# A graph layer on one core: groups of six edges, one-hots of 128 columns, and fields turned a row later

## The chip, the cores and the metric

The kernel runs on one core of a Trainium2 chip. The metric is the device time of one execution in microseconds (us). The core has a matrix engine (TensorE, PE in the profile, with its weight loads listed apart as PEld), a vector engine (VectorE, DVE), a scalar engine (ScalarE, ACT), GpSimd (POOL) and a queue engine (SyncE, SP). Each engine runs its own instructions in order and waits on semaphores for the others.

## The reference

There are 625 nodes with 512 numbers each, and 20,625 edges, sorted by the node they end at (`dst`), each with a source node, one of four types and a weight.

```python
h = relu(layernorm(x))
xs = h[src]
for r in range(4):
    w_r = where(edge_type == r, edge_weight, 0.0)
    total_msg += (xs @ W_rel[r] + b_rel[r]) * w_r[:, None]
agg = segment_sum(total_msg, dst) / maximum(segment_sum(edge_weight, dst), 1.0)
x1 = layer_norm(h + h @ W_self + b_self + agg, ln1_g, ln1_b)
ffn = gelu(x1 @ W_ffn1 + b_ffn1) @ W_ffn2 + b_ffn2
out = x + layer_norm(x1 + ffn, ln2_g, ln2_b)
```

The feed-forward layer is 512 to 1024 to 512.

## The kernel before

**Table.** The 625 nodes are five blocks of 125. For each type `r` and block `i`, `table_rows(r, i)` (L366) multiplies the block's 125 rows of `h` by `W_rel[r]`: four f32 matmuls of 128x128 by 128x512, each done as two passes and so shown as two records. ScalarE scales the result (L374) and a DMA on SP's queue writes it to a table in DRAM (L376). There are 4 x 5 = 20 such rows of the table; the loop over `(r, i)` runs through them in order. What is to be summed for a node is then a weighted sum of rows of this table.

**Two ways to sum.** For blocks 0, 1 and 2 (called outer or dense) the weights are made into a dense matrix: `turn_fields(d)` (L597) turns the edges' fields of outer block `d` with five bf16 matmuls against an identity; `slot_hots(d, u)` makes, on VectorE, the one-hot matrices of a unit of 16 slots: `low` (L614; which of 125 rows, with one more column of ones, so 126 columns), `eq` (L617) and `high` (L620, three of them). `slot_sums` (L631) multiplies `low` by `high`: a bank is four matmuls, each with a weight load of its own (126 columns that stand 8 elements of bf16 apart, so 16 bytes) and 120 moving columns. `empty_sums` (L637) adds a bank up into `sums_w` on VectorE. An outer block has 4 units of 4 banks: 12 units, 48 banks and 192 matmuls in all. `chunk_sum` (L1043) then multiplies `sums_w` by table rows, 20 for each outer block; nine of them are kept in SBUF and eleven are read back from DRAM (`tr`, two to a load).

For blocks 3 and 4 (called inner) the table's rows are gathered edge by edge. `gather` (L919) is an indirect DMA on GpSimd's queue that brings 128 table rows of 2 KB to 128 partitions. Edges of the inner part are put into groups of 128 x EG, where each partition holds EG edges that follow one another, so nearly always edges of one node. The first of the EG gathered rows is scaled by ScalarE into PSUM (`first_row`, L925), the others are added by VectorE (`row_added`, L943), and the sum goes through one matmul with a one-hot of the destination node (`edge_sum`). This matmul is in plain f32 (two passes, L966), or, for a parted sum, two faster matmuls of a high and a low half (L963, L964) after one more operation on ScalarE (`high`, L929) and one on VectorE (`low`, L933). Where a partition holds edges of two nodes, the later ones are left out and added from a second gather for the inner block's nodes: EG - 1 gathers for a block (`gather_first`, L973; `add_first`, L969).

**Order.** In the first part (the loop over `(r, i)`) the order is written out by hand: units of `slot_hots` are interleaved with rows of the table, up to `PER_ROW` = 3 banks behind a row; `EARLY` units are done there, the rest later. In the second part `Plan` orders the work: a list scheduler that runs at build time on costs in the code (a gather is 1.3, a bank 0.33, a pause of GpSimd after every `RUN` = 4 gathers 0.5) and emits a fixed order for each engine. It places the products with `W_self` (`pz`, L386), the chunk sums, the edge sums, the layer norms, the transposes (L319) and the feed-forward matmuls (`pu` L714, `po` L732). The feed-forward layers run in the order of blocks 0, 1, 3, 2, 4. At most `MS` = 8 gathered tiles, two PSUM tiles for edge groups (`add`) and six `es` tiles are there at a time.

The diff touches these places: the constant `EG`; the tiles `lows` and their constant fill (L292); the matmul of `slot_sums`; the constants `PARTED`, `FIRST_AT` and `EARLY`; and the conditions in the loop over `(r, i)` that say behind which row the fields are turned and the weights of the slots and the degrees are made.

Of the kernel before, what the change touches and what calls it, by code (L numbers as in the profile page):

```python
# [12 lines left out]
BF16 = mybir.dt.bfloat16  # L13
# [1 line left out]
ALU = mybir.AluOpType  # L15

P = 128
EG = 3
SLOTS = 64


class EdgePlan:
# [3 lines left out]
    def __init__(self, n_nodes, n_tiles, n_free, nb):  # L26
# [21 lines left out]
        tiles = [j for j in range(n_tiles) if window[j][1] > n0 and window[j][0] < n1]  # L48
        self.groups = -(-len(tiles) // EG)
        self.group0 = min(tiles[0], n_tiles - EG * self.groups)  # L50
        self.limits = [(0, b0 * P) if j < self.group0 else ((b1 + 1) * P, nb * P) for j in range(n_tiles)]
        self.of_sum = {}
        for k in range(self.groups):
            unit = list(range(self.group0 + EG * k, self.group0 + EG * (k + 1)))
            lo, hi = self.row(window[unit[0]][0]), self.row(window[unit[-1]][1] - 1)
# [3 lines left out]
            else:  # L59
                limits = (bs[0] * P + P // 2, bs[1] * P + P // 2)  # L60
                assert len(bs) == 2 and limits[0] <= lo and hi < limits[1]
            self.limits[unit[0]:unit[-1] + 1] = [limits] * EG
            self.of_sum.setdefault(bs, []).append(unit)
# [73 lines left out]
def gnn_layer(ctx, tc, x, edges, edge_groups, firsts, fourths, windows, w_self, w_rel, w_ffn1, w_ffn2, brel_in, rows_in, bf1_in, out, n_edges):  # L137
# [12 lines left out]
    nc = tc.nc  # L150
# [10 lines left out]
    NG = ep.each  # L161
# [7 lines left out]
    SL = windows.shape[1] // 4  # L169
# [11 lines left out]
    mid = ctx.enter_context(tc.tile_pool(name="mid", bufs=1))  # L181
# [71 lines left out]
    xw = const.tile([P, 4, INNER], F32, name="xw")  # L253
    x_cols = const.tile([P, INNER, EG, 3], F32, name="x_cols")
    x_on = const.tile([P, INNER, EG - 1], F32, name="x_on")
    x_step = const.tile([P, INNER, EG, 2], F32, name="x_step")
# [14 lines left out]
    TB = 8  # L271
    TP = 2
# [1 line left out]
    grid = mid.tile([P, NG, TB], BF16, name="grid")  # L274
    keys = mid.tile([P, 2 * NC, TP], BF16, name="keys")
    ident_b = early.tile([P, P], BF16, name="ident_b")
    lows = [mid.tile([P, SL // 4 // TB, NG + 1, TB], BF16, name=f"low_{n}") for n in range(2)]

    def node_constants():
        place = early.tile([P, 1], F32, name="place")  # L280
        nc.gpsimd.iota(place, pattern=[[0, 1]], base=0, channel_multiplier=1, allow_small_or_imprecise_dtypes=True)
        nc.gpsimd.memset(node_f, 2.0 * N)
        nc.gpsimd.memset(xw, -1.0)
        for b in range(NB):
            n = ep.size[b]
            nc.vector.tensor_scalar(node_f[:n, at_of[b]:at_of[b] + 1], place[:n], float(ep.first[b]), None, op0=ALU.add)
            if b in inner:
                nc.vector.tensor_scalar(xw[:n, 0, b - B0:b - B0 + 1], place[:n], float(b * P), None, op0=ALU.add)
        nc.gpsimd.iota(keys, pattern=[[1, 2 * NC], [0, TP]], base=0, channel_multiplier=0,
                       allow_small_or_imprecise_dtypes=True)  # L290
        for t in lows:
            nc.gpsimd.memset(t[:, :, NG:, :], 1.0)  # L292
        nc.gpsimd.iota(grid, pattern=[[1, NG], [0, TB]], base=0, channel_multiplier=0,
                       allow_small_or_imprecise_dtypes=True)

# [294 lines left out]
    QT = 4  # L590
    UNIT = SL // 4
# [31 lines left out]
    def slot_sums(d, u, q, low, high, place):  # L623
        if (d, u, q) == (d, 0, 0):
            sums_w[OUTER[d]] = const.tile([P, NC, P], F32, tag="sums_w", name=f"sums_w{d}", bufs=2)
        pool, tag = place
        p = pool.tile([P, D], F32, tag=tag, name=f"bank_{d}_{u}_{q}")
        W = 3 * 2 * NC
        for i in range(QT):
            t = q * QT + i  # L630
            nc.tensor.matmul(p[:NG + 1, i * W:(i + 1) * W], low[:, t // TB, :, t % TB], high[:, t // TP, :, t % TP],  # L631
                             start=True, stop=True)
        return p

# [160 lines left out]
    PAUSE = 200  # L795
    RUN = 4
    LATER = 0.3
    PARTED = 1, 2
    LA = 3
    CH = 2  # L800
    FIRST_AT = (2, 3)
    units = [(d, u) for d in range(ND) for u in range(SL // UNIT)]
    EARLY = 7
    PER_ROW = 3
    with tc.manual_schedule(engines={PE, DVE, ACT, mybir.EngineType.Pool}):
        nc.scalar.activation(gelu_of, ones, AF.Gelu)
        node_constants()
        stats = x_stats(0)

        def next_norm(i):  # L810
            nonlocal stats
            if i < NB:
                pre_norm(i, stats)
            if i + 1 < NB:
                stats = x_stats(i + 1)

        warm = ps_one.tile([P, D], F32, tag="one", name="warm")
        for _ in range(WARM):
            nc.tensor.matmul(warm, zeros[:, :P], zeros, start=True, stop=True)
        next_norm(0)  # L820
        for k, n in ((0, 1), (1, 1), (2, 2)):
            transposed(hT[0][:, k:k + n, :], z[:, 0, k * P:(k + n) * P], f"h0_{k}")
        next_norm(1)
        hots, waiting, later, sums_now = {}, units[:EARLY], [], []
        for r in range(R):
            for i in range(NB):
                def next_transposed():
                    transposed(hT[i + 1], z[:, i + 1, :], f"h{i + 1}")
                    next_norm(i + 2 if i == 0 else i + 3)

                table_rows(r, i, next_transposed if r == 0 and i + 1 < NB else None)
                for d, u, q in sums_now:
                    p = slot_sums(d, u, q, *hots[d, u], ((ps_one, "one"), (ps_acc, "acc"), (ps_add, "add"), (ps_add, "add"))[q % 4])
                    empty_sums(d, u, q, p)
                sums_now = [later.pop(0) for _ in range(min(PER_ROW, len(later)))]
                if r == 0 and i < 3:
                    if i == 0:
                        next_norm(3)
                        find_tiles()
                    rows_of_tiles(2 * i, min(2 * i + 2, NB))  # L840
                if (r, i) == (0, 3):
                    find_windows()
                if (r, i) == (1, 0):
                    edge_columns()
                if (r, i) == (1, 1):
                    slot_weights(0, ND)
                    slot_fields()
                if (r, i) == (1, 4):
                    slot_weights(ND, NB)
                    slot_degrees()  # L850
                    degrees_turned = relation_degrees()
                if (r, i) == (2, 2):
                    degrees_turned()
                if (r, i) >= (1, 3) and waiting and len(later) + len(sums_now) <= UNIT // QT:
                    d, u = waiting.pop(0)
                    if d not in turned_fields:
                        turn_fields(d)
                    hots[d, u] = slot_hots(d, u)
                    later += [(d, u, q) for q in range(UNIT // QT)]
                if (r, i) == (1, NB - 1):  # L860
                    group_columns()
                if r == 3 and i < KD:
                    nc.vector.tensor_add(ws_sb[:, i, i * P:(i + 1) * P], ws_sb[:, i, i * P:(i + 1) * P], ident)
                if (r, i) == (3, 0):
                    for g_bc in (g1_bc, g2_bc):
                        nc.vector.tensor_scalar(g_bc, g_bc, 1.0 / RS, None, op0=ALU.mult)
                if (r, i) == FIRST_AT:
                    first_edges()
                    load_first_edges()
                if (r, i) == (2, NB - 1):  # L870
                    set_limits(0)
                    set_limits(1)
                    total_outside = count_outside()
            later_loads(r)
        assert not waiting
        for d, u, q in sums_now + later:
            p = slot_sums(d, u, q, *hots[d, u], ((ps_one, "one"), (ps_acc, "acc"), (ps_add, "add"), (ps_add, "add"))[q % 4])
            empty_sums(d, u, q, p)
        for d in range(ND):
            if d not in turned_fields:  # L880
                turn_fields(d)
# [101 lines left out]
    g_last, g_before, n = None, None, 0  # L983
# [62 lines left out]
    m, ld, t, here = {b: None for b in OUTER}, None, None, {}  # L1046
# [19 lines left out]
    stay, i = list(range(NC - KEPT, NC)), 0  # L1066
    for d, b in enumerate(OUTER):
        weights_of(d)
        order = (*stay, *range(NC - KEPT)) if d != 1 else (*range(NC - KEPT), *stay)
        for c in order:  # L1070
            if c not in stay and (b, c) not in here:
                n = min(CH, NC - KEPT - c)
# [8 lines left out]
            if i == 8:  # L1081
                t = op("PE", 0.1, lambda: total_outside(), after=[m[b], first_ready], take=["ps"], give=["ps"], lag=2.0, rank=(2, 2.085))
# [15 lines left out]
    for b in range(NB):  # L1098
# [3 lines left out]
        for name, eng, us, fn, needs in steps:  # L1102
# [4 lines left out]
        p = [None]  # L1107
        t = op("PE", 0.46, lambda got=got, p=p, b=b: p.__setitem__(0, turn(got["x1"], f"x1_{b}")),
               after=[made["x1"]], take=["ps"], give=["ow"], rank=(1,))
# [5 lines left out]
    for blocks in together:  # L1115
        members, n = [], 0
# [177 lines left out]
```

## Time and profile before

| | |
|---|---|
| median of 3 runs | 303.15 us (300.43 to 304.28) |
| profiled execution | 304.07 us, of which the profile's span is 302.2 us |
| PE busy | 283.5 us (94% of the span) |
| DVE busy | 188.5 us (62%) |
| POOL busy | 102.3 us (34%) |
| ACT busy | 60.1 us (20%) |
| DMA | 47.94 MB, 159 GB/s over the span |
| mean granted TensorE clock | 0.977 |

The profile is of one execution. Its groups of instructions give for a line the count, the busy time and the mean duration; matmuls overlap, so the mean of one is longer than the distance between two. The chain of waits follows the work that ended last back through what released it; there, pieces of work stand end to end.

### The profile page before, as it was taken

Reading aid. Unit: us, or ns where it says so; the run is one execution under the profiler, and the core shown is the slowest. Engines: PE = TensorE matmul, PEld = TensorE weight load, DVE = VectorE, ACT = ScalarE, POOL = GpSimd, SP = SyncE. Lnnn points to the kernel's source line nnn. Section 1 sums busy time; section 2 is a strip of 40 time slices with the busy share of each in tenths; the row PEclk is TensorE's granted clock in tenths of the full one; section 3 lists DMA queues with packets and bytes.
Section 4 is the critical chain, followed back from the end, with each engine's and each line's share of the span. In section 5 each row is a group of like instructions: output and inputs, shape, how many; then the busy total and the mean of one; then the engine's idle time right before and its main releaser. Section 6 shows DMA issues by size and latency. Waiting matters only on the chain.

```text
span 302.2 us, 3190 instructions
## 1 busy us (share of the span) xinstructions
PE 283.5 (94%) x1047; PEld 174.3 (58%) x1047; DVE 188.5 (62%) x440; ACT 60.1 (20%) x115; POOL 102.3 (34%) x146
## 2 busy tenths in 40 slices
PE   7999949999999999999697979999999999999991
PEld 3444414776677575644263745685954456686870
DVE  5613179677594678974686739697979650650614
ACT  2331120111210020212021202032532001121230
POOL 6161500000300008777777474742777110000000
PEclk9999987999999999999999979999999999999997
DMA  7759765852111139668999998551567332001011
GB/s 236 293 150 342 252 210 216 313 206 63 39 36 50 49 110 282 176 170 221 297 258 291 286 257 242 150 170 35 152 193 196 120 100 72 2 0 34 2 36 37
DMA packets 19972, 47.94 MB, mean 159 GB/s; under 512 B 2351, under 2 KB 3065, under 8 KB 19824
## 3 DMA queue, kind: packets, MB, share of 16 engines
q1 hardware_dynamic: 13348, 27.54, 28.1%
q0 software_dynamic: 6304, 19.89, 23.2%
q10 hardware_dynamic: 300, 0.26, 0.4%
q8 instruction: 9, 0.15, 0.2%
q14 instruction: 11, 0.09, 0.1%
HBM read 41.29 MB, written 6.52 MB: 158 GB/s over the span
## 4 chain that ended last, share of the span: by engine, by line
PE 73%; DMA 12%; DVE 6%; issue 4%; POOL 3%; SPq 1%; DVEq 0%; POOLq 0%
PE acc L1043 14%; PE pt L366 14%; PE bank L631 12%; PE pu L714 12%; PE po L732 11%; PE pz L386 5%; DMA tr<-table 4%; DMA ms<-table,row_i 4%; PE acc L966 3%; DMA xs<-in_x_dram 2%; DMA win<-in_windows_dram,at_i 2%; POOL dst L462 2%; PE acc L960 1%; POOL win L462 1%; PE acc L964 1%
## 5 line engine op out<-in xcount | busy, mean ns | idle before, releaser
L919 POOL DMA_INDIRECT ms<-table,row_i x69 | 69.0, 1000 | 70.6 <-DVE eq L617 33.7
L366 PE MATMUL pt<-wr,hT 128*128 128x512 f32 x160 | 74.4, 614 | 0.2
L631 PEld LDWEIGHTS <-low 128*126 128x126 bf16 x192 | 48.5, 321 | 9.9 <-issue 6.4
L637 DVE TENSOR_REDUCE sums_w<-bank 126x160 f32<-126x480 f32 x48 | 31.2, 656 | 30.7 <-PE bank L631 30.7
L366 PEld LDWEIGHTS pt<-wr,hT 128*128 128x128 f32 x160 | 30.3, 197 | 33.3 <-issue 32.8
L631 PE MATMUL bank<-high,low 128*126 128x120 bf16 x192 | 44.3, 367 | 0.0
L714 PE MATMUL pu<-x1T,w_sb 128*128 128x125 f32 x320 | 37.8, 276 | 0.0
L714 PEld LDWEIGHTS pu<-x1T,w_sb 128*128 128x128 f32 x320 | 36.9, 192 | 1.4 <-issue 1.4
L1043 PE MATMUL acc<-tr,sums_w 126*128 126x512 f32 x66 | 32.7, 626 | 3.7 <-DMA tr<-table 3.7
L732 PE MATMUL po<-w_sb,gT 128*125 128x512 f32 (+2 forms) x96 | 35.7, 521 | 0.0
L925 ACT ACTIVATE ea<-ms,ed 128x512 f32<-128x512 f32 x23 | 15.9, 691 | 60.6 <-DMA ms<-table,row_i 33.4
L943 DVE SCALAR_TENSOR_TENSOR ea<-ms,wgt_g,ea 128x512 f32<-128x512 f32 x31 | 22.9, 747 | 8.0 <-DMA ms<-table,row_i 6.6
L374 ACT ACTIVATE m<-pt,rx 125x512 f32<-125x512 f32 x20 | 13.7, 687 | 70.5 <-PE pt L366 60.4
L732 PEld LDWEIGHTS po<-w_sb,gT 128*125 128x125 f32 x96 | 16.5, 188 | 15.2 <-issue 13.0
L1043 PE MATMUL acc<-m,sums_w 126*128 126x512 f32 x54 | 25.2, 596 | 0.0
L718 ACT ACTIVATE gT<-pu,bf 128x125 f32<-128x125 f32 x40 | 14.7, 366 | 46.2 <-PE pu L714 46.2
L1043 PEld LDWEIGHTS acc<-tr,sums_w 126*128 126x128 f32 x66 | 12.4, 199 | 16.3 <-issue 11.6
L740 DVE TENSOR_TENSOR y<-po,z 125x512 f32<-125x512 f32 (+2 forms) x6 | 3.6, 603 | 24.2 <-PE po L732 24.2
L386 PE MATMUL pz<-ws_sb,hT 128*128 128x512 f32 x40 | 18.1, 596 | 0.0
L1043 PEld LDWEIGHTS acc<-m,sums_w 126*128 126x128 f32 x54 | 10.0, 191 | 10.2 <-issue 10.1
L555 POOL DMA_INDIRECT x_edges<-in_edge_groups_dram,x_group x2 | 1.9, 944 | 41.2 <-DVE x_group L551 40.9
L620 DVE TENSOR_TENSOR high<-eq,turned 128x640 bf16<-128x640 bf16 x36 | 15.5, 487 | 0.4
(168 smaller groups left out, 243.2 us busy)
## 6 DMA issues: line engine op xcount, KB each, us to landing
tr<-table SPq DMA_DIRECT2D x15, 504.0 KB
table<-m SPq DMA_DIRECT2D x20, 250.0 KB
w_sb<-in_L_gnn_W_ffn_dram SPq DMA_DIRECT2D x2, 2048.0 KB
wr<-in_L_gnn_W_rel_dram SPq DMA_DIRECT2D x3, 1024.0 KB
rows<-in_rows_dram SPq DMA_DIRECT2D x1, 1536.0 KB
ms<-table,row_i POOLq DMA_INDIRECT x69, 4.1
ws_sb<-in_L_gnn_W_self_dram SPq DMA_DIRECT2D x1, 1024.0 KB
out_dram<-y SPq DMA_DIRECT2D x4, 224.0 KB
```

Of the source, the lines that this page charges most:

```text
L366: nc.tensor.matmul(p, hT[i][:, k, :], wr_sb[r][:, k, :], start=(k == 0), stop=(k == KD - 1))
L386: nc.tensor.matmul(p[0], hT[i][:, k, :], ws_sb[:, k, :], start=(k == 0), stop=(k == KD - 1))
L620: nc.vector.tensor_mul(high[:, :, a * 2 * NC:(a + 1) * 2 * NC, :], eq, pairs(2 + a))
L631: nc.tensor.matmul(p[:NG + 1, i * W:(i + 1) * W], low[:, t // TB, :, t % TB], high[:, t // TP, :, t % TP], start=True, stop=True)
L637: nc.vector.tensor_reduce(sums_w[OUTER[d]][:NG + 1, :, n0:n0 + 2 * QT].rearrange("p c (t h) -> p t h c", h=2), p[:NG + 1, :QT * 3 * 2 * NC ...
L714: nc.tensor.matmul(pu[:, :nn], w1_sb[:, k, f * P:(f + 1) * P], x1T_b()[:, k, :nn], start=(k == 0), stop=(k == KD - 1))
L718: nc.scalar.activation(box["gT"][:, f, :nn], pus[f][:, :nn], AF.Gelu, bias=bf1[:, f:f + 1])
L732: nc.tensor.matmul(po[h][:n, :w], box["gT"][:, f, at], w2_sb[:, f, c], start=(f == 0), stop=(f == KF - 1))
L919: nc.gpsimd.indirect_dma_start(out=ms[j], out_offset=None, in_=table[:, :], in_offset=bass.IndirectOffsetOnAxis(ap=row_i[:, j:j + 1], axis=0))
L925: nc.scalar.activation(box["sum"], ms[j], AF.Copy, scale=wgt[:, j:j + 1])
L943: nc.vector.scalar_tensor_tensor(to, ms[j], wgt_g[:, k, q - 1:q], box["sum"], op0=ALU.mult, op1=ALU.add)
L1043: nc.tensor.matmul(acc[b,], sums_w[b][:NG + 1, c, :], kept[(b, c) if (b, c) in kept else c][:NG + 1], start=first, stop=last)
```

## The change

Groups have six edges to a partition instead of three. `low` has 128 columns: 125 one-hot columns, one of ones, and two of zeros that are written once; the matmul takes all 128. The first fields are turned behind row (1, 4) of the table instead of (1, 3), the slot weights of the inner blocks and the degrees move from behind (1, 4) to behind (2, 0), their turned degrees from (2, 2) to (2, 3), and the first edges from (2, 3) to (2, 2). Six units instead of seven are done in the first part. The rule for parted sums changes from every second one with at least three behind it to every one with at least three behind it.

```diff
-EG = 3
+EG = 6
...
-    lows = [mid.tile([P, SL // 4 // TB, NG + 1, TB], BF16, name=f"low_{n}") for n in range(2)]
+    lows = [mid.tile([P, SL // 4 // TB, P, TB], BF16, name=f"low_{n}") for n in range(2)]
...
         for t in lows:
-            nc.gpsimd.memset(t[:, :, NG:, :], 1.0)
+            nc.gpsimd.memset(t[:, :, NG:NG + 1, :], 1.0)
+            nc.gpsimd.memset(t[:, :, NG + 1:, :], 0.0)
...
-            nc.tensor.matmul(p[:NG + 1, i * W:(i + 1) * W], low[:, t // TB, :, t % TB], high[:, t // TP, :, t % TP],
+            nc.tensor.matmul(p[:, i * W:(i + 1) * W], low[:, t // TB, :, t % TB], high[:, t // TP, :, t % TP],
                              start=True, stop=True)
...
-    PARTED = 1, 2
+    PARTED = 1, 1
     LA = 3
     CH = 2
-    FIRST_AT = (2, 3)
+    FIRST_AT = (2, 2)
     units = [(d, u) for d in range(ND) for u in range(SL // UNIT)]
-    EARLY = 7
+    EARLY = 6
...
                 if (r, i) == (1, 1):
                     slot_weights(0, ND)
                     slot_fields()
-                if (r, i) == (1, 4):
+                if (r, i) == (2, 0):
                     slot_weights(ND, NB)
                     slot_degrees()
                     degrees_turned = relation_degrees()
-                if (r, i) == (2, 2):
+                if (r, i) == (2, 3):
                     degrees_turned()
-                if (r, i) >= (1, 3) and waiting and len(later) + len(sums_now) <= UNIT // QT:
+                if (r, i) >= (1, 4) and waiting and len(later) + len(sums_now) <= UNIT // QT:
```

`PARTED` is read by `parted(k, units)`: `k % PARTED[1] < PARTED[0] and k + 3 < len(units)`, where `units` are the groups that go to one accumulator. The groups of the inner part are 23 before (11, 2 and 10 in the three accumulators) and 12 after (6, 1 and 5).

## Prediction

> **What bounds the kernel now.** I read the engines' shares first, then the chain of waits, then its pieces in order of time.
>
> ```profile
> PE 283.5 (94%) x1047; PEld 174.3 (58%) x1047; DVE 188.5 (62%) x440; ACT 60.1 (20%) x115; POOL 102.3 (34%) x146
> PE 73%; DMA 12%; DVE 6%; issue 4%; POOL 3%; SPq 1%; DVEq 0%; POOLq 0%
> ```
>
> TensorE carries the end. A busy TensorE is not one at its peak, so the pieces of the chain, which stand end to end, give the real cost of each step (start, length, what):
>
> ```profile
> 44.16 0.29 PE tf L597
> 44.44 9.47 PE pt L366 x16
> 53.91 2.59 PE bank L631 x12
> 56.50 3.49 PE pt L366 x8
> ...
> 102.83 3.49 PE pt L366 x8
> 106.32 3.52 PE bank L631 x16
> 109.83 0.28 PE tf L597 x5
> ...
> 195.56 0.74 PE bank L631 x4
> ...
> 227.57 0.23 PE acc L963
> 227.80 0.23 PE acc L964
> ...
> 242.24 0.86 PE acc L966 x2
> ```
>
> A table row is 3.49 us. A bank of four matmuls is 0.86 (2.59 / 3) in a run of three and 0.74 alone: 0.19 to 0.22 us for a weight load and a matmul with 120 columns. The five turns of the fields, which also load 128 columns of bf16 each and stream 128, take 0.28, so 0.056 apiece. The cost of a bank is thus its weight load, not its stream. Between 44.4 and 109.8 the chain is table rows and banks alone: 28 banks, 24.1 us.
>
> The rows of the windows show the parts (length from A to B, then busy time of PE, PEld, DVE, ACT and POOL):
>
> ```profile
> 44.16:110.11 65.95, 65.95 (x214) 44.39 (x215) 45.35 (x100) 9.60 (x16) 2.48 (x9) 0.96 0.35 122
> 110.11:242.30 132.19, 125.98 (x444) 75.51 (x443) 100.88 (x210) 28.08 (x52) 82.22 (x107) 0.99 0.72 205
> 242.30:295.53 53.23, 53.20 (x288) 37.31 (x286) 19.47 (x53) 11.45 (x28) 1.01 (x1) 1.00 0.12 35
> 295.53:302.20 6.67, 0.00 (x0) 0.00 (x0) 2.94 (x10) 0.20 (x1) 0.00 (x0) 0.73 0.15 42
> ```
>
> In the second, the gathers run beside TensorE. Their issues in the timeline of GpSimd:
>
> ```profile
> 112.74 1.25 POOL L919 DMA_INDIRECT ms<-table,row_i  x1 [33.70 <-DVE eq L617]
> ...
> 160.29 0.95 POOL L919 DMA_INDIRECT ms<-table,row_i  x1 [0.16 <-issue]
> ...
> 211.17 0.95 POOL L919 DMA_INDIRECT ms<-table,row_i  x1 [2.37 <-DVE ea L943]
> ...
> 234.05 0.95 POOL L919 DMA_INDIRECT ms<-table,row_i  x1 [0.16 <-issue]
> ```
>
> Numbered from 1 these are the 33rd at 160.29, the 57th at 211.17 and the 73rd, the last. The pace is 1.49 us (47.55 / 32) where nothing holds them, 2.12 (50.88 / 24) in the middle, where they wait for gathered tiles to come free, and 1.68 (121.3 / 72) over all.
>
> **The change part by part.**
>
> *One-hots of 128 columns.* The weight load is what a bank costs, and it changes from 126 columns to 128, 16 bytes apart as before. No row has a load of 128 columns at that distance. The bounds: 0.225 us for a bank, as for the turned fields, whose columns stand close together, and 0.86, no change. Below 0.225 the stream of 120 columns leaves no room, since the turns' 0.056 is for 128. I take 0.225: the same type, the same count of columns, and f32 loads of 128 columns are hidden under the matmuls in the table rows, so no load of full width shows a cost here, and only that of 126 does. The two more zero fills on GpSimd, 16 columns each, stand before the first x has landed, which the start waits for: nothing.
>
> [...]
>
> *Fields turned a row later.* TensorE stands before the turns, in its timeline:
>
> ```profile
> 32.46 6.60 PE L366 MATMUL pt<-wr,hT 128*128 128x512 f32 x15
> 41.87 0.23 PE L597 MATMUL tf<-ident_b,fields 128*128 128x128 bf16 x1 [2.81 <-DVE fields L515]
> 44.16 0.29 PE L597 MATMUL tf<-ident_b,fields 128*128 128x128 bf16 x1 [0.30 <-DVE fields L522]
> ```
>
> From 39.06 to 44.16 it does four small turns and waits for VectorE, whose chain stays as it is. A table row of 3.49 goes into this gap whole: -3.49. The 16 records behind it took 9.47 instead of 6.98, at a lower granted clock; up to 2.5 more could be won if the shorter gap leaves the clock alone, and I count none of it.
>
> *First part, summed.* 28 banks at 24.1 become 24 at 5.4 (-18.7), one row less (-3.49): its end moves from 110.11 to 87.9. VectorE must follow. Its work in this window is 45.35; a unit less takes off 2.97 for the one-hots (35.6 / 12) and 2.6 for four sums:
>
> ```profile
> L637 DVE TENSOR_REDUCE sums_w<-bank 126x160 f32<-126x480 f32 x48 | 31.2, 656 | 30.7 <-PE bank L631 30.7
> L620 DVE TENSOR_TENSOR high<-eq,turned 128x640 bf16<-128x640 bf16 x36 | 15.5, 487 | 0.4
> L614 DVE TENSOR_TENSOR low<-turned,grid 128x2000 bf16<-128x2000 bf16 x12 | 14.3, 1193 | 1.8 <-ACT turned L600 1.8
> L617 DVE TENSOR_TENSOR eq<-turned,keys 128x640 bf16<-128x640 bf16 x12 | 5.8, 485 | 0.0
> ```
>
> 39.8 is left and could start at 45.4: 85.2 without a wait, so VectorE nearly becomes the bound here, and behind each `empty_sums` waits a PSUM tile for the next bank. I allow 1 us: 88.9. The last table row has 22 banks ahead of it instead of 24: its end moves from 106.32 to 106.32 - 3.49 - 20.6 + 5.0 + 1 = 88.2. The first gather came 6.42 after it and does so again: 94.6. The steps moved behind other rows (slot weights, degrees, first edges) issue the same instructions; their two loads of first edges on GpSimd stand before any gather, with its queue idle, and cost nothing.
>
> *Six edges to a partition.* 23 groups become 12, so 69 gathers 72; each inner block needs 5 extra gathers instead of 2. 73 become 82, all on GpSimd's queue. VectorE adds 60 rows instead of 46 and 10 first rows instead of 4, at 0.75; parted sums go from 8 to 5 (3 of 6, 0 of 1, 2 of 5):
>
> ```profile
> L943 DVE SCALAR_TENSOR_TENSOR ea<-ms,wgt_g,ea 128x512 f32<-128x512 f32 x31 | 22.9, 747 | 8.0 <-DMA ms<-table,row_i 6.6 <-ACT ea L925 1.2
> L933 DVE TENSOR_TENSOR el<-ea,eh 128x512 fp32r<-128x512 f32 x8 | 5.5, 683 | 0.7 <-ACT eh L929 0.7
> L966 PE MATMUL acc<-es,oh 128*128 128x512 f32 x30 | 15.4, 594 | 0.0
> ```
>
> VectorE: 20 x 0.747 - 3 x 0.683 + 5.6 (the unit put off) = +18.5 on the second part, 100.9 to 119. TensorE: 15 plain sums become 7 (-8 x 0.86), three parted fewer (-3 x 0.46): -8.3. ScalarE does 11 first rows and three parts fewer and isn't near a bound.
>
> *The rest of TensorE.* 20 banks at 0.74 become 24 at 0.225: -9.4. Its work behind the first part is 125.98 + 53.20 - 8.3 - 9.4 = 161.5.
>
> *What ends last.* From the first gather, 81 distances are to be made: 120.7 at 1.49, 136.1 at 1.68. The slow middle came while TensorE was full and held the tiles; now it has room, but VectorE has 119 us of work in some 140. I take the middle, 128.4: the last issue is at 223.0. Before, VectorE had added its last row 5.5 after the last issue (239.6), and the edge sum takes 0.86: 229.4. In the built order five stretches and a turn stand behind this last edge sum: two `pu` and three `po`, as these rows, and the turned block 4 in the first:
>
> ```profile
> 274.57 6.87 PE po L732 x16
> 281.44 7.14 PE pu L714 x64
> 288.59 6.92 PE po L732 x32
> 295.53 0.30 DVE y L740
> ```
>
> 6.87 + 0.44 + 7.14 + 6.87 + 7.14 + 6.92 = 35.4, where before 52.4 stood behind it. The norm of block 4 hides under the first `po`; without that cover it would cost up to 6. End of TensorE 264.8, and the 6.67 after it: 271.5, so 30.7 less than the span of 302.2. The profiled run was 304.07, 1.87 more than its span, and 0.92 over the median: 272.4, said as 272.
>
> **The rivals.**
>
> *TensorE stays the bound.* Gathers at 1.49 and nothing waiting: 88.9 + 161.5 + 6.7 = 257.1, as a time 258. For it: it is full now. Against it: 94.6 + 120.7 + 6.4 + 35.4 + 6.7 is already 263.8.
>
> *The 128 columns don't do it.* If the distance of 16 bytes and not the count makes the load slow, banks stay at 0.86. The first part ends at 110.11 - 3.49 - 4 x 0.86 = 103.2, the last row at 101.1, the first gather is at 107.5, and the same sum from there (128.4 + 6.4 + 35.4 + 6.7) gives 284.4, as a time 285. For it: no row has a full load at this distance. Still faster, since the row and the shorter tail stay.
>
> *VectorE's chain of five adds holds the gathers: slower.* A group now keeps its PSUM tile through one scaling and five adds in order, with eight gathered tiles to hold, and in VectorE's order every add that waits for a landing holds the norms, one-hots and bank sums behind it. If the middle pace, 2.12, then holds all through: 94.6 + 171.7 + 6.4 + 35.4 + 6.7 = 314.8, as a time 316. It decides from a pace of 1.96, which ends at 302. For it: 119 us of VectorE's work, and a DMA share of 0.72 that 9 more gathers raise in less time. Against it: the 1.49 pace was held for 32 distances while VectorE was fullest.
>
> **How the numbers follow.** The forecast of 272, with 264 to 280 for paces of 1.49 to about 1.68, has 0.5; TensorE as the bound 0.12; no faster load 0.2; the slower rival 0.1, most of it above 303; the rest, 0.08, lies between. The range goes from 258, where TensorE is the bound, to 290, which takes in banks at 0.86 with a pace a little slower than the middle; it leaves some 0.15 to 0.2 out, nearly all above. Two per cent, 6 us, is about what can be told from no change here. Faster 0.84 (forecast, the first two rivals and part of the rest), within it 0.06, slower 0.10.
>
> **What would show it.** In the profile after: loads of `low` in the form 128x128 and four of them to a bank in some 0.23 us of the chain; the last table row at about 88 and the first gather at about 95; 82 gathers, the last near 223; VectorE busy some 201 us (188.5 + 14.9 - 2.0); the last plain edge sum followed by 35 us of feed-forward. A bank still at 0.86 would be the second rival, a first gather at 95 with a last one beyond 250 the third.

## The result and the profile after

The kernel after takes 284.76 us in the median (284.12 to 285.58, four runs) beside 302.6 for the kernel before: a ratio of 0.942 with a 95% interval of 0.935 to 0.948. It is faster by 17.8 us where the forecast was 31. The profiled execution has a span of 282.3. In this and the later runs, ratios and their intervals leave out executions over 1.5% longer than the fastest of their kernel, while medians and the ranges in brackets hold all of them.

The page of the kernel after, engine shares and the chain of waits by engine:

```profile
PE 251.5 (89%) x1025; PEld 140.0 (50%) x1025; DVE 195.2 (69%) x455; ACT 51.3 (18%) x101; POOL 115.2 (41%) x157
PE 48%; DMA 16%; DVE 15%; issue 10%; POOL 5%; SPq 1%; ACT 1%; another core or an unknown queue 1%; DVEq 0%; ACTq 0%; POOLq 0%
```

TensorE lost 32 us of busy time and no longer carries the end alone: its part of the chain went from 73% to 48%, and transfers, VectorE and GpSimd together have 36% of it instead of 21%. The windows of the kernel after (the gap before the turned fields; the rest of the first part; the part with the gathers; what stands behind the last edge sum; the last steps of VectorE and the store). As before, a row gives start and end, length, the busy times of PE, PEld, DVE, ACT and POOL, the granted clock, the DMA share and GB/s:

```profile
39.06:44.17 5.11, 4.10 (x14) 1.66 (x12) 4.77 (x16) 1.37 (x2) 0.00 (x0) 1.00 0.59 193
44.17:87.20 43.03, 42.12 (x190) 22.38 (x191) 38.17 (x90) 8.92 (x15) 3.06 (x9) 1.00 0.50 181
87.20:240.52 153.32, 132.36 (x529) 73.31 (x529) 118.95 (x248) 22.66 (x47) 94.41 (x116) 0.94 0.72 200
240.52:275.92 35.40, 35.37 (x196) 25.25 (x195) 15.29 (x40) 7.95 (x19) 1.00 (x1) 1.00 0.07 23
275.92:282.30 6.38, 0.00 (x0) 0.00 (x0) 2.94 (x10) 0.20 (x1) 0.00 (x0) 0.79 0.15 44
```

The first part takes 43 us instead of 66. In the third window TensorE stands still for 21 us of 153; before, it stood still for 6 of 132. Behind the last edge sum it is full again, for the 35.4 us that the order puts there.

The chain's pieces of the kernel after show what a bank costs now, and the end:

```profile
65.22 0.74 PE bank L632 x12
65.96 3.49 PE pt L367 x8
...
82.92 3.49 PE pt L367 x8
86.41 0.26 PE bank L632 x4
...
144.61 0.40 PE bank L632 x4
...
239.66 0.86 PE acc L967 x2
240.52 6.87 PE po L733 x16
...
268.98 6.92 PE po L733 x32
275.92 0.30 DVE y L741
```

Three banks take 0.74, so some 0.245 each instead of 0.86; the bank of 0.40 ran at a granted clock of 0.50. The last table row ends at 86.41. The first and the last of the 82 gathers:

```profile
93.79 1.69 POOL L920 DMA_INDIRECT ms<-table,row_i  x1 [26.63 <-DVE x_on L573]
...
230.04 0.95 POOL L920 DMA_INDIRECT ms<-table,row_i  x1 [0.30 <-issue]
```

That is 81 distances in 136.25 us: 1.68 each, the pace of before to the second digit.

### The profile page after: what moved, and what is told of

Read it like the earlier page. It is cut to its first block, busy times and chain, and to the rows that moved or that the text cites. A ratio compares the mean times of both kernels' runs of the same rounds, so it can differ in the third digit from the quotient of the medians.

```text
span 282.3 us, 3166 instructions
## 1 busy us (share of the span) xinstructions
PE 251.5 (89%) x1025; PEld 140.0 (50%) x1025; DVE 195.2 (69%) x455; ACT 51.3 (18%) x101; POOL 115.2 (41%) x157
## 4 chain that ended last, share of the span: by engine, by line
PE 48%; DMA 16%; DVE 15%; issue 10%; POOL 5%; SPq 1%; ACT 1%; another core or an unknown queue 1%; DVEq 0%; ACTq 0%; POOLq 0%
PE pu L715 13%; PE po L733 10%; PE acc L1044 10%; DMA ms<-table,row_i 9%; PE pt L367 9%; DVE ea L944 3%; DMA tr<-table 3%; PE bank L632 3%; DMA xs<-in_x_dram 2%; PE acc L967 2%; POOL ms L920 2%; DMA win<-in_windows_dram,at_i 2%; DVE sums_w L638 2%; POOL dst L463 2%; DVE high L621 1%
## 5 line engine op out<-in xcount | busy, mean ns | idle before, releaser
L920 POOL DMA_INDIRECT ms<-table,row_i x72 | 74.2, 1031 | 63.1 <-DVE x_on L573 26.6
L367 PE MATMUL pt<-wr,hT 128*128 128x512 f32 x160 | 71.7, 597 | 0.0
L944 DVE SCALAR_TENSOR_TENSOR ea<-ms,wgt_g,ea 128x512 f32<-128x512 f32 x53 | 39.2, 748 | 22.8 <-DMA ms<-table,row_i 14.6
L367 PEld LDWEIGHTS pt<-wr,hT 128*128 128x128 f32 x160 | 29.5, 192 | 31.8 <-issue 31.3
L1044 PE MATMUL acc<-tr,sums_w 126*128 126x512 f32 x66 | 34.9, 661 | 3.0 <-DMA tr<-table 2.5
L638 DVE TENSOR_REDUCE sums_w<-bank 126x160 f32<-126x480 f32 x48 | 29.9, 650 | 8.4 <-PE bank L632 3.6
L632 PEld LDWEIGHTS <-low 128*128 128x128 bf16 x192 | 17.5, 147 | 19.6 <-issue 18.9
L375 ACT ACTIVATE m<-pt,rx 125x512 f32<-125x512 f32 x20 | 13.8, 688 | 55.1 <-PE pt L367 46.4
L926 ACT ACTIVATE ea<-ms,ed 128x512 f32<-128x512 f32 x12 | 8.3, 692 | 82.4 <-DMA ms<-table,row_i 58.8
L632 PE MATMUL bank<-high,low 128*128 128x120 bf16 x192 | 17.7, 226 | 2.8 <-DVE z L391 1.9
L615 DVE TENSOR_TENSOR low<-turned,grid 128x2000 bf16<-128x2000 bf16 x12 | 14.3, 1190 | 1.3 <-ACT turned L601 1.3
```

The source lines that it names most:

```text
L367: nc.tensor.matmul(p, hT[i][:, k, :], wr_sb[r][:, k, :], start=(k == 0), stop=(k == KD - 1))
L615: nc.vector.tensor_tensor(low[:, :, :NG, :], of[:, 0].rearrange("p (a t) -> p a t", t=TB).unsqueeze(2).to_broadcast([P, nb_, NG, TB]), gri ...
L632: nc.tensor.matmul(p[:, i * W:(i + 1) * W], low[:, t // TB, :, t % TB], high[:, t // TP, :, t % TP], start=True, stop=True)
L638: nc.vector.tensor_reduce(sums_w[OUTER[d]][:NG + 1, :, n0:n0 + 2 * QT].rearrange("p c (t h) -> p t h c", h=2), p[:NG + 1, :QT * 3 * 2 * NC ...
L920: nc.gpsimd.indirect_dma_start(out=ms[j], out_offset=None, in_=table[:, :], in_offset=bass.IndirectOffsetOnAxis(ap=row_i[:, j:j + 1], axis=0))
L944: nc.vector.scalar_tensor_tensor(to, ms[j], wgt_g[:, k, q - 1:q], box["sum"], op0=ALU.mult, op1=ALU.add)
```

## The experiments

Theory G said that in the kernel after the gather stream sets the end: its first issue, its pace, and the matmuls that the order puts behind the last edge sum. Its rival P said that TensorE's sum still does. The first four runs split the change. The second part's order is planned anew for every kernel: edits of the columns leave it alone (52.4 us of matmuls stand behind the last edge sum in `cols_only`, as in the kernel before, and 35.4 in `after_126`, as in the kernel after), while edits of the edges, the pauses or the tiles also move other steps.

**128 columns alone** (`cols_only`: the kernel before with the wider one-hots):

```diff
-    lows = [... [P, SL // 4 // TB, NG + 1, TB] ...]
+    lows = [... [P, SL // 4 // TB, P, TB] ...]
...
-            nc.gpsimd.memset(t[:, :, NG:, :], 1.0)
+            nc.gpsimd.memset(t[:, :, NG:NG + 1, :], 1.0)
+            nc.gpsimd.memset(t[:, :, NG + 1:, :], 0.0)
...
-            nc.tensor.matmul(p[:NG + 1, ...], low[...], high[...],
+            nc.tensor.matmul(p[:, ...], low[...], high[...],
```

> The kernel before with one part of the change: the one-hots have 128 columns; three edges to a partition and the old order stay. A bank should cost 0.245 us as in the kernel after instead of 0.86, so 28 banks in the first part give 17.2 us back and the first gather comes near 95.5. Theory G (the gather stream sets the end: 72 distances at 1.68, then 9 to the last edge sum, 52.4 of matmuls that stand behind it in the order, and 6.7): a span of 284.6, a time near 286. Rival P (TensorE's sum sets the end: 92.9 for the first part, 169 of work behind it, some 6 of waits, 6.7): a time near 276.

Measured: 280.95 us (278.76 to 284.81) beside 302.45. There is no interval for its ratio, but its highest time lies 15 us below the lowest of the kernel before. Its gathers, in an execution of 278.81 us:

```profile
98.23 0.95 POOL L920 DMA_INDIRECT ms<-table,row_i  x1 [25.93 <-DMA tr<-table]
...
210.19 0.95 POOL L920 DMA_INDIRECT ms<-table,row_i  x1 [0.16 <-issue]
```

72 distances at 1.56. The first issue came 2.7 later than expected, the pace was better than G's 1.68 and worse than the 1.49 where nothing held it; the time lies between G's 286 and P's 276. One part of the change brings about as much as the whole of it, and perhaps more: the profiled execution lies 5 us below all those of the kernel after, the highest of the four among them. Without an interval that isn't settled here, but the run with three edges below points the same way.

**Six edges alone** (`six_only`: the kernel before with `EG = 6`):

> The kernel before with one part of the change: six edges to a partition instead of three; 126 columns, the old order and every second sum parted stay. Theory G: first gather still near 112.7, 81 distances at 1.68, 10.5 to the last edge sum, 36.2 of matmuls behind it, 6.4: a span of 302, no change. Rival P: TensorE loses some 8 us of edge sums, a time near 295.

Measured: 296.41 us, ratio 0.980 (0.972 to 0.989). P's 295 was near and G's 302 was not: with slow banks 6 of the 8 us that TensorE's edge sums lose arrive. That TensorE is the bound there is P's reading of the number; the only profile of this kernel is of an execution of 303.06 us, and by G's own sum a gather stream at 1.59 instead of 1.68 would give this time as well, so it isn't shown.

**The kernel after with 126 columns** (`after_126`) has the edit of `cols_only` undone and all else as in the kernel after:

> The kernel after with the 128 columns undone (126, banks at 0.86 expected, up from 0.245). Theory G: the first gather moves by 22 banks, from 93.8 to 107.3, and everything behind it with it (81 distances at 1.68, 10.5, 35.4, 6.4): a span of 296, a time near 298. Rival P: all 48 banks count on TensorE, 48 x 0.6 = 29 us: a time near 313.

Measured: 294.01 us, ratio 0.972 (0.964 to 0.981). Fast banks are worth 9 us here, while alone they are worth 21 by the medians. Its gathers and its last edge sum:

```profile
106.14 0.95 POOL L919 DMA_INDIRECT ms<-table,row_i  x1 [37.20 <-DVE x_cols L563]
...
238.36 0.95 POOL L919 DMA_INDIRECT ms<-table,row_i  x1 [0.30 <-issue]
...
249.58 0.86 PE acc L966 x2
```

The first gather is 12.4 us later than in the kernel after and the last only 8.3: the pace is 1.63 instead of 1.68. G was nearer (298 expected, P 313), with a pace that isn't fixed; what makes it better here no run takes apart.

**The kernel after with three edges** (`after_eg3`):

```diff
-EG = 6
+EG = 3
```

> The kernel after with three edges to a partition again, all else as after. Theory G: first gather at 93.8, 72 distances instead of 81 at 1.68, 8 to the last edge sum, 46.4 of matmuls behind it in this order, 6.5: a span of 276, a time near 278, so the six edges cost 7 us beside the fast banks. Rival P: TensorE gets 5.5 us more of edge sums on top of its 87.2 + 167.8: with the same waits as after (21 us) a time near 290, so the six edges gain.

Measured: 275.73 us (274.39 to 277.95), ratio 0.912 (0.905 to 0.919): below the kernel after, whose interval it doesn't touch, by about 9 us. G's 278 was right in its sign and within 3; P's 290 was wrong. So six edges, worth 6 us on the kernel before, cost 9 in the kernel after (a later pair of runs turns this sign round again). Its gathers are 73:

```profile
94.07 1.63 POOL L920 DMA_INDIRECT ms<-table,row_i  x1 [26.61 <-DMA tr<-table]
...
212.96 0.95 POOL L920 DMA_INDIRECT ms<-table,row_i  x1 [0.44 <-issue]
```

The start and the pace (1.65) are those of the kernel after; nine distances fewer at nearly the same pace make the last issue 17 us earlier. The order gives some of it back with 46.4 instead of 35.4 behind the last edge sum.

**What makes the weight load fast** was asked by two runs of one execution each. `after_127` takes 127 of the 128 columns out of the same tile, and `before_close` puts the 126 columns of the kernel before side by side:

```diff
-            nc.tensor.matmul(p[:, ...], low[:, t // TB, :, t % TB], ...)
+            nc.tensor.matmul(p[:P - 1, ...], low[:, t // TB, :P - 1, t % TB], ...)
```

> The kernel after, but the matmul of a bank takes 127 of the 128 columns; the tile, its 16-byte distance and all else stay. If the count of exactly 128 makes the load fast: a bank back at 0.74 to 0.86 us and a time near that with 126 columns, 294. If the cost only grows or falls with the columns or with the place of the row in the tile: a bank near 0.245, a time near 285.

```diff
-    lows = [... [P, SL // 4 // TB, NG + 1, TB] ...]
+    lows = [... [P, SL // 4 // TB, TB, NG + 1] ...]
...
-        nc.vector.tensor_tensor(low[:, :, :NG, :], ...
+        nc.vector.tensor_tensor(low[:, :, :, :NG].rearrange("p a t n -> p a n t"), ...
...
-            ... low[:, t // TB, :, t % TB] ...
+            ... low[:, t // TB, t % TB, :] ...
```

> The kernel before with 126 columns that stand side by side (2 bytes) instead of 16 bytes apart; VectorE writes them across, so its one-hots may take longer. If the distance made the load slow: a bank near 0.25 us. If the count of 126 did: a bank still at 0.74 to 0.86. The time is not what is asked, as VectorE's cost moves it too.

With 127 columns the time was 294.12, that of 126 columns, and the chain shows

```profile
52.08 2.62 PE bank L632 x12
```

0.87 for a bank. With 126 columns side by side the groups and the chain's pieces show

```profile
L631 PEld LDWEIGHTS <-low 128*126 128x126 bf16 x192 | 18.9, 157 | 67.2 <-issue 38.4 <-DVE high L620 19.1 <-DVE low L614 9.5
L614 DVE TENSOR_TENSOR low<-turned,grid 128x2000 bf16<-128x2000 bf16 x12 | 106.1, 8844 | 1.3 <-ACT turned L600 1.3
...
175.34 0.24 PE bank L631 x4
```

0.24 for a bank, as fast as with 128. Three others in this chain take 0.42 to 0.58; ahead of those of 0.43 and 0.42 two f32 matmuls take 1.71 instead of the usual 0.86. Over all 192, a load takes 157 ns in the mean, beside 147 with 128 columns in the kernel after and 321 in the kernel before. Neither the count nor the distance alone made a load slow in these runs: with the columns 16 bytes apart a bank took 0.245 at 128 columns, 0.87 at 127 and 0.86 at 126, and with 126 side by side 0.24. The time of `before_close`, 363.33, shows why the columns don't simply stand side by side: VectorE writes such a one-hot in 8.84 us instead of 1.19.

The drop from 0.87 to 0.245 between 127 and 128 columns, 16 bytes apart, is 3.5 times for load and matmul together. Why 126 columns are slow at that distance (0.86) while 128 are not (0.245), no run here shows.

**What holds the gathers** was asked by two edits of the kernel after: no pauses of GpSimd (`after_no_pause`), and ten tiles for gathered rows with four for sums to make room (`after_ms10_es4`).

```diff
-    RUN = 4
+    RUN = 1000
```

> The kernel after without the pauses of GpSimd behind every fourth gather (16 of some 0.6 us and the gap beside them); the build-time order shifts a little, 38.0 us of matmuls stand behind the last edge sum instead of 35.4. Theory T1 (the gathers wait for their eight tiles to come back): the pace stays at 1.68 us a gather, a time of 284 to 287. Theory T3 (GpSimd's own rate sets the pace): 1.4 to 1.5 a gather, the last issue 15 us earlier, a time near 272. Theory T4 (the transfers' own rate, with the read-back loads beside them): no gain, landings later, a time of 284 to 290.

```diff
-    MS = 8
-    ES = 6
+    MS = 10
+    ES = 4
```

> The kernel after with ten tiles for gathered rows instead of eight (and four es tiles instead of six, to fit); 38.0 us of matmuls stand behind the last edge sum. T1: the pace goes from 1.68 towards 1.49 us, up to 15 us earlier at the last issue, a time of 270 to 277. T3 and T4: the pace stays, a time of 284 to 288.

Measured: 274.8 us, ratio 0.915 (0.905 to 0.925), and 276.49 us, ratio 0.914 (0.897 to 0.932). Both gain, the first as T3 said (GpSimd's own rate) and the second as T1 said (the tiles), so both were in the way, and T4, the transfers' rate as the only limit, falls. The gathers and the last edge sum without pauses:

```profile
95.17 1.76 POOL L920 DMA_INDIRECT ms<-table,row_i  x1 [26.56 <-DMA tr<-table]
...
217.00 0.94 POOL L920 DMA_INDIRECT ms<-table,row_i  x1 [0.30 <-issue]
...
227.68 0.86 PE acc L967 x2
```

81 distances at 1.50: the last issue is 13 us earlier, the last edge sum 12, the span 9 (273.4), since 38.1 instead of 35.4 stand behind it. With ten tiles the pace is 1.56, in a profiled execution of 278.44 us.

GpSimd's timelines show what each edit took away. Waits of over 1.1 us before a gather, all put down to a step of ScalarE or VectorE that uses gathered rows, sum to 16.8 us in the kernel after (six waits), 16.0 without the pauses (seven) and 8.3 with ten tiles (three). So without the 17 pauses the waits for tiles are nearly what they were, and with two more tiles they are half. Not everything gave way: from the 33rd to the 49th gather the pace is 1.91 in the kernel after and 1.87 in both of these, and what holds that stretch stays open.

**The order and the parted sums.** `after_old_order` undoes the moved steps, `after_parted2` the rule for parted sums:

```diff
-    FIRST_AT = (2, 2)
-    EARLY = 6
+    FIRST_AT = (2, 3)
+    EARLY = 7
...
-                if (r, i) == (2, 0):
+                if (r, i) == (1, 4):
                     slot_weights(ND, NB)
...
-                if (r, i) == (2, 3):
+                if (r, i) == (2, 2):
                     degrees_turned()
-                if (r, i) >= (1, 4) and waiting and ...
+                if (r, i) >= (1, 3) and waiting and ...
```

> The kernel after with the order of the kernel before: fields turned behind row (1, 3), seven units in the first part, and the moved steps back; 128 columns, six edges and the parted sums stay. The table row of 3.49 us no longer fills the gap before the turned fields, and two more banks (0.5) stand ahead of the last row: the first gather moves from 93.8 to near 97.8; the work behind the last edge sum in this order is 42.9 us instead of 35.4. If the gather stream sets the end: 97.8 + 136.3 + 10.5 + 42.9 + 6.4, a time near 295. If only the row counts: 284.8 + 3.5, near 288.

```diff
-    PARTED = 1, 1
+    PARTED = 1, 2
```

> The kernel after with every second sum parted again (three parted, nine plain): TensorE gets 0.8 us more, VectorE 1.4 and ScalarE 1.2 less; 39.8 us of matmuls stand behind the last edge sum instead of 35.4. If the gather stream sets the end, the order counts: a time of 285 to 289. If VectorE's load holds the gathers, it gains: below 284.

Measured: 292.62 us, ratio 0.959 (0.947 to 0.971), so the new order is worth some 5 us in the kernel after (0.959 less 0.942, of 301); the intervals just touch, so its size is uncertain, and the expected 3.5 of the row and 10 of the whole stream lie on its two sides. The parted sums gave 286.19 (282.33 to 291.81), a range that holds that of the kernel after: no effect is shown.

**Three edges without pauses** (`eg3_no_pause`) and with ten tiles on top (`eg3_no_pause_ms10`) put the gains together:

```diff
-EG = 6
-    RUN = 4
+EG = 3
+    RUN = 1000
```

> The kernel after with three edges to a partition and without GpSimd's pauses. If the gather stream still sets the end (first gather 94, 72 distances at 1.50 as in the kernel of six edges without pauses, 8, 48.1, 6.5): a time near 267. If TensorE takes over as the bound (87.2 + some 173 of work, 6.5): 269 or more, up to 274, little below the 275.7 with pauses.

```diff
-    MS = 8
-    ES = 6
+    MS = 10
+    ES = 4
```

> The kernel after with three edges to a partition, no pauses and ten tiles for gathered rows (four es tiles). If the gather stream sets the end: a pace below 1.4, the last issue near 195, a time of 258 to 262. If TensorE is the bound: 266 to 272, no gain over the same kernel with eight tiles.

Measured: 286.69 us, ratio 0.953 (0.942 to 0.963), and 289.5 us, ratio 0.958 (0.946 to 0.971). Both theories missed. Taking out the pauses makes three edges 11 us slower, where it makes six edges 10 faster: without pauses six edges are 12 us better than three (274.8 beside 286.69), the reverse of what the kernel after and `after_eg3` show. The gathers of `eg3_no_pause`:

```profile
94.07 1.63 POOL L920 DMA_INDIRECT ms<-table,row_i  x1 [26.61 <-DMA tr<-table]
...
214.74 0.94 POOL L920 DMA_INDIRECT ms<-table,row_i  x1 [0.30 <-issue]
...
208.40 10.31 DMA tr<-table
```

The pace is 1.68 though no pause is left: the waits of over 1.1 us are 24.9 here (eight) beside 11.6 in `after_eg3` (three). The last piece, from its chain, shows TensorE's line held for 10 us by a read-back load. The pauses are steps of the build-time plan, so taking them out moves every later step of the order as well; whether the waits come from that new order or from gathers and read-back loads that now meet was not taken apart, and stays open.

## Why the prediction was right, and where it was too large

**The bank: right.** 0.245 instead of the 0.225 taken; 22 banks make 0.4 us. Its reading, that the load and not the stream is the cost, was right (a load took 321 ns in the mean before and 147 after, with the same 120 columns streamed); its reason, that no load of full width shows a cost, was incomplete, as in `before_close` a load of 126 shows none either (0.24 for a bank). For a load of 128 columns 16 bytes apart it had no row, as it said; `after_127` shows that at this distance the count decided between 127 (0.87) and 128 (0.245).

**The row in the gap: right, and the clock with it.** The kernel after in TensorE's timeline:

```profile
44.17 0.23 PE L598 MATMUL tf<-ident_b,fields 128*128 128x128 bf16 x1 [0.36 <-DVE fields L523]
44.27 7.11 PE L367 MATMUL pt<-wr,hT 128*128 128x512 f32 x16
```

The 16 records behind the turns take 7.11 instead of 9.68 and the granted clock is 1.00 in both windows from 39.06 on, where it was 0.74 over these records before (44.44 to 53.91): the 2.5 us that were not counted came. They more than paid for the waits on VectorE's sums near 56, 0.9 us, for which 1 us had been allowed. The last row ended at 86.41 (88.2 predicted), the first gather was at 93.79 (94.6).

**VectorE's added work: right in its terms, and in its window partly by luck.** 118.95 us in the window of the gathers, 119 predicted. But 4.2 of that had stood behind the last edge sum before (19.47 there, 15.29 now), which the prediction did not count. In all it was 195.2, where 201 was said. By the groups of VectorE, the adds and parted sums grew by 12.8, as predicted; one-hots of the destination nodes and bank sums, not in the sum, fell by 2.9, and about as much again is durations that overlap in the busy time (the groups' sums exceed it by 16.3 before and 19.3 after).

**The pace: the step that failed.** "The slow middle came while TensorE was full and held the tiles; now it has room" gave the middle between 1.49 and 1.68; it was 1.68, which makes the last issue 7 us late (230.04 for 223.0). TensorE had room and the tiles were held all the same. That TensorE's fullness had not been the cause could be read from windows of the kernel before, cut where the pace changes:

```profile
112.70:161.30 48.60, 46.08 (x130) 24.47 (x128) 37.37 (x79) 8.40 (x13) 37.08 (x49) 1.00 0.85 237
161.30:212.10 50.80, 47.10 (x193) 31.69 (x193) 36.84 (x76) 9.91 (x19) 27.54 (x34) 0.97 0.69 199
212.10:235.00 22.90, 22.90 (x103) 14.98 (x102) 19.75 (x42) 8.24 (x17) 17.60 (x25) 1.00 0.68 187
```

TensorE was busy for 95% of the quick first stretch (1.49), 93% of the slow middle (2.12) and 100% of the last, which was quick again (1.43, 22.88 / 16). VectorE, too, was fullest in the last stretch (86%, against 77% in the first), not in the first, as the prediction said against the third rival. One place in the kernel after where gathers are held, in the timelines of GpSimd, VectorE and TensorE, then in the chain, then as a window:

```profile
119.78 0.95 POOL L920 DMA_INDIRECT ms<-table,row_i  x1 [3.53 <-ACT ea L926]
135.59 1.42 DVE L944 SCALAR_TENSOR_TENSOR ea<-ms,wgt_g,ea 128x512 f32<-128x512 f32 x2 [7.42 <-DMA ms<-table,row_i]
139.68 0.79 PE L964 MATMUL acc<-eh,oh 128*128 128x512 f32 x1 [7.97 <-issue]
...
126.89 1.02 POOL ms L920
...
128.67 8.83 DMA ms<-table,row_i
...
138.26 0.65 DVE ea L944
...
118.80:143.80 25.00, 13.75 (x38) 6.21 (x37) 13.75 (x23) 3.17 (x5) 17.11 (x23) 0.85 0.89 237
```

A gather waits 3.5 for a use of gathered rows by ScalarE, which puts back those behind it; one issued at 128.67 lands 8.8 later, while the DMA engines are busy at 0.89; VectorE stands 7.4 before an add whose rows have not landed, with all that follows in its order behind it, and TensorE stands 8.0 before the edge sum of that group. Both are busy for 13.75 us of these 25, and the granted clock is 0.85 in their mean, and 0.50 from 139.0 to 145.2, behind TensorE's wait. These are the waits of the third rival, adds behind a landing in VectorE's order, at 1.68 and not at its 2.12; where the prediction set it against "TensorE has room", the two were not alternatives. That the chain of five adds makes these waits is not shown: with two adds to a group the pace is 1.65 (`after_eg3`). What is shown is that the pauses and the number of tiles each count; how much of the rest is the planned order, VectorE's load or the transfers stays open.

**From the last gather to the last edge sum: mis-sized.** 6.4 was taken, 10.5 was measured. VectorE's last add starts at 236.28 behind steps of a norm and ends at 237.0, 7.0 after the last issue; TensorE's order has a stretch of `pu` there, from 233.41 to 239.66 in its chain, and the edge sum comes behind it. I had taken VectorE's 5.5 us of before and left out what TensorE's order puts in front, though 9 us from the last issue to the end of the last edge sum could be read from the trace of before (234.05 to 243.10).

**The tail: right.** 35.40 us measured, 35.4 predicted; 6.4 after it. The two errors, 7.0 and 4.1, less 0.3 of the end, are the 10.8 by which the span is over 271.5. So the band of 264 to 280, which was to take in a pace of 1.68, was missed by 4.8 us: the pace alone would have ended near 280, and the term behind the last gather did the rest.

**The rivals.** TensorE as the bound fits the time of six edges on slow banks (`six_only`), and not the kernel after, which it put at 258. The second, banks that stay at 0.86, was given 285 and came at 294 (`after_126`), by the same two mis-sized terms; that the kernel after then took the time forecast for that rival was chance. The whole was foreseen as faster and came within its range, but the prediction did not ask whether six edges still pay once banks are fast. In the kernel after they don't: the same kernel with three is 9 us faster. Without GpSimd's pauses they do, by 12.

## What to carry to other kernels

An edit that moves work from the bound to an engine that only has time to spare need not pay once that bound has gone. Cost each part again with the others done: six edges were worth 6 us on the old kernel, cost 9 beside fast banks and were worth 12 there without the pauses. Where an order is planned at build time, a part's worth belongs to that order.

For a stream that is held by few buffers, take the pace that was measured over its whole length (1.68 here, before and after), not the one where nothing held it (1.49), until an edit of the buffers or of the issuing engine shows otherwise. And measure from the last transfer to the end of its last use, in the order in which the engines will take it (10.5 us here, for which 6.4 had been taken).

## What the hardware showed that I had not expected

A bf16 weight load of 126 or 127 columns 16 bytes apart took 0.19 to 0.22 us with its short matmul (the kernel before, `after_127`); of 128 at the same distance (the kernel after, 0.245 for four), or of 126 side by side (`before_close`, 0.24 for four), both together took 0.06. VectorE took 7.4 times as long (8.84 us in `before_close` against 1.19) to write the same one-hot with the other order of its axes.
